# A transformer block on one core: expert multiplications, DMA issues and value products are put in another order within a step

## The chip, the core and the metric

The kernel runs on one core of one Trainium2 chip. The metric is the time of one execution on the device, in microseconds (us). TensorE (PE in the profile) multiplies matrices and loads its weights (PEld), VectorE (DVE), ScalarE (ACT) and GpSimd (POOL) work on tiles, and SyncE (SP) issues nearly all DMA transfers from one queue, in program order.

## The reference

The input x is 2 x 128 x 256 x 256 in fp32 (images, channels, rows, columns). Cut to what matters:

```python
x = x + conv(_ln_c(x))          # attention between windows
t = _to_tokens(x)               # one token for each pixel, 128 channels
t = t + ffn(_ln_t(t))           # mixture of experts

# conv: q, k, v = 1x1 convolutions (128 channels, 4 heads of 32); each 8x8 window of queries
# looks at the 12x12 window of keys around it; a mask of -inf leaves only the keys whose row
# and column offsets are of one parity; relative position logits are added
attn = softmax(q*SCALE @ k.T + rel_pos_emb(q*SCALE) + FIXED_MASK)
out  = W_out @ (attn @ v)

# ffn
router_probs = softmax(x @ router_w + router_b)      # 8 experts
top_p, top_i = top_k(router_probs, 2);  top_p /= sum(top_p)
expert_out   = einsum('bnd,edc->bnec', x, expert_w) + expert_b
out          = sum over the two chosen experts of top_p * expert_out
```

## The kernel before, in words

**Tiles.** The two images are cut into 64 strips of 8 rows. Because of the mask, queries of one parity of row and column meet only keys of that parity, so each strip splits into four planes (row parity, column parity). One step n of the main loop (line 654) handles one plane: `i, pl = divmod(n, 4)`. There are 256 steps with attention, and seven more in which the last expert work runs out.

**What a step does.** A step weaves together work of several planes and rows through generators, each `next` issuing one piece:
- `scores(n)`: position logits (L371), then scores for half of the windows (L388), then the other half, then the exponentials on ScalarE (L396). These are 32 and twice 64 short matmuls of 32 rows by 64 columns.
- `attend(n)`: the sums of the exponentials by ones (L409, 16 matmuls), the value products (L417, 128 short matmuls), then on VectorE the chain that divides by the sums: a transpose `sT` (L427), reciprocals `rc` (L429), a second transpose `rT` (L432), and the product `o` (L437).
- `out_project(n)`: `po` (L445) on TensorE, then its addition to x on VectorE (L450), the other operand being in PSUM.
- `project(n + 1)`: two copies of windows on POOL (`xcol`, L290), q (`pq`, L296), position terms (`pu`, L306, with transposes on VectorE), keys (`pk`, L325), and the values in two groups of four windows (`pvv`, L342).
- `norms` and `route` for one pair of rows (512 tokens) whose attention is finished, and `norms` for the first layer norm of a later row: transposes (`px_f`, `px_c`, L214), router logits (`plt`, L469), statistics and a chain of small VectorE operations up to the gates `g` (L535).
- `spread`: the gates are transposed (`pg`, L542), copied by ScalarE (`gT`), stored to DRAM (`gd`, L546), and read back from there as broadcasts to all 128 partitions: `rb` (L550) for the layer norm, which POOL applies in the next step (`ln1`, L264), and one `gb` of 256 KB for each expert.
- `Experts`: for each of the 8 experts, `times(e)` multiplies the rows by the broadcast gate (`xe`, L580; experts 3 and 7 on POOL, the others on VectorE) and `product(e)` adds the expert's product to the accumulator (`acc`, L585, two matmuls of 128 x 512). `end` adds the expert biases (L591) and adds the sum to x (L592); the fourth row pair of a strip also stores the strip (L612, 1 MB). Every fourth step loads a strip (L104, 1 MB).

**What sets the order.** The five engines' orders are written out by hand (`tc.manual_schedule`): what is issued first in the program comes first on its engine. The module function `times(ex, nxt, e)` issues expert e's multiplication for the rows `ex` and, behind it, the fetch of the broadcast of the same expert for the following rows `nxt`:

```python
    def times(ex, nxt, e):
        ex.times(e, pool if e % 4 == 3 else dve)
        nxt.fetch(e)
```

The fetch goes into the one buffer that the multiplication frees (`gb`, 8 buffers for 8 experts), so SP waits for the multiplication before it issues the fetch, and everything behind it in SP's queue waits too. `xe` has 6 buffers, so a multiplication waits for the product that read its buffer six multiplications earlier. In the step before the change SP's order is: the strip's load (every fourth step), `gb2`, `gb4`, `gb7`, `gb5`, `gb6`, `gd`, `rb`, `gb0`, `ge`, `gb1`, `gb3`, the strip's store (every fourth step).

Of the kernel before, what the change touches and what calls it, by code (L numbers as in the profile page):

```python
# [10 lines left out]
F32 = mybir.dt.float32  # L11
# [5 lines left out]
P = 128  # L17
# [28 lines left out]
def kernel(  # L46
# [21 lines left out]
    HP = NP // 2  # L68
# [3 lines left out]
    NT = CH // P  # L72
# [5 lines left out]
    work = ctx.enter_context(tc.tile_pool(name="work", bufs=2))  # L78
# [20 lines left out]
    def load_x(i):  # L99
        if i >= len(strips):  # L100
            return
        b, s = strips[i]
        xt[i] = xpool.tile([P, R, W], F32, tag="xt", name=f"xt{i}")
        nc.sync.dma_start(xt[i], x[b, :, s * R : (s + 1) * R, :])  # L104
# [295 lines left out]
    def attend(n, state):  # L400


        att, pT, vv = state["att"], state["pT"], state["vv"]
        av = att[:, :, HQ:512]
        for half in range(2):
            rows = slice(half * SLOT, (half + 1) * SLOT)
            for h in range(HEADS):
                hp = slice(h * DH, (h + 1) * DH)
                nc.tensor.matmul(  # L409
                    av[hp, 2 + half], lhsT=ones[rows, :], rhs=pT[rows, h], start=True, stop=True  # L410
                )
        for t in range(HP):
            for half in range(2):
                rows = slice(half * SLOT, (half + 1) * SLOT)
                for h in range(HEADS):
                    hp = slice(h * DH, (h + 1) * DH)
                    nc.tensor.matmul(  # L417
                        av[hp, half, 32 * t : 32 * t + 32],
                        lhsT=vv[rows, t, hp],
                        rhs=pT[rows, h, 32 * t : 32 * t + 32],  # L420
                        start=True,
                        stop=True,
                    )


        sT = work.tile([P, 2, HQ], F32, tag="sT", name=f"sT{n}", bufs=1)
        nc.vector.transpose(sT, av[:, 2:4])  # L427
        rc = small.tile([P, NQ // 32], F32, tag="rc", name=f"rc{n}")
        nc.vector.reciprocal(rc, sT.rearrange("p f (b k) -> p (f b) k", k=32)[:, :, 0])  # L429
        yield  # L430
        rT = work.tile([P, 2, HQ], F32, tag="rT", name=f"rT{n}", bufs=1)
        nc.vector.transpose(  # L432
            rT.rearrange("p f (b k) -> p (f b) k", k=32),
            rc.unsqueeze(2).broadcast_to([P, NQ // 32, 32]),
        )
        o = work.tile([P, 2, HQ], F32, tag="o", name=f"o{n}")
        nc.vector.tensor_tensor(o, av[:, 0:2], rT, ALU.mult)  # L437
        state["o"] = o
        yield
# [117 lines left out]
    class Experts:  # L557
# [18 lines left out]
        def times(self, e, eng):  # L576

            nm = "_".join(str(v) for v in (*self.at, e))
            self.xe[e] = work.tile([P, NT * P], F32, tag="xe", name=f"xe{nm}", bufs=6)
            eng.tensor_tensor(self.xe[e], self.src, self.gb.pop(e), ALU.mult)  # L580

        def product(self, e):
# [6 lines left out]
        def end(self):  # L589

            nc.tensor.matmul(self.acc, lhsT=eb, rhs=self.ge, start=False, stop=True)  # L591
            nc.vector.tensor_add(self.src, self.acc, self.src)  # L592
            i, k = self.at
            if k == R // 2 - 1:
                store(i)

    class NoExperts:
        def fetch(self, e):
# [7 lines left out]

        def end(self):
            pass

    def store(i):  # L610
        b, s = strips[i]
        nc.sync.dma_start(out[b, :, s * R : (s + 1) * R, :], xt.pop(i))  # L612
# [38 lines left out]

    ET = mybir.EngineType
    with tc.manual_schedule(engines={ET.PE, ET.DVE, ET.Activation, ET.Pool, ET.SP}):
        for n in range(n_planes + 7):
            i, pl = divmod(n, 4)
            live = n < n_planes
            if pl == 0:
                load_x(i + 3)
            score, attn, outp, ahead, norm, rout = none, none, none, none, none, none
            if live:  # L660
                score = scores(n, states[n])
# [12 lines left out]
            ex.product(0)  # L674
            next(score, None)
            next(ahead, None)
            times(ex, nxt, 2)
            made = next(norm, None)
            next(score, None)
            if f:  # L680
# [4 lines left out]
            next(rout, None)  # L685
            next(ahead, None)
            next(ahead, None)
            times(ex, nxt, 4)
            next(rout, None)
            if pl == 3 and i + 2 < len(strips):  # L690
                halo(i + 2)
            ex.product(1)
            times(ex, nxt, 7)
            next(attn, None)
            next(attn, None)
            if row:
                ln1(*row, pool)
            ex.product(2)
            ex.product(3)
            times(ex, nxt, 5)  # L700
            next(ahead, None)
            ex.product(4)
            next(outp, None)
            times(ex, nxt, 6)
            next(outp, None)
            next(ahead, None)
            ex.product(5)
            for c1 in cs[1:]:
                ln1_now(*c1)
            row, new = None, NoExperts()  # L710
            if made:
                gd, row = spread(f, c, made[0], f"_{n}")
                row = (*c, row) if c else None
                new = Experts(*f, gd) if f else new
            ex.product(6)
            ex.product(7)
            for e in (0, 1, 3):
                times(nxt, new, e)
            ex.end()
            ex, nxt = nxt, new  # L720
# [59 lines left out]
```

## Time and profile before

| what | value |
|---|---|
| median of 3 runs | 5573.74 us (5567.08 to 5577.78) |
| the profiled execution's own time | 5572.79 us |
| its span, first to last instruction | 5571.0 us |
| mean granted TensorE clock | 0.973 |
| busy: PE, DVE, ACT, POOL | 94%, 78%, 23%, 28% |
| DMA | 763.81 MB, mean 137 GB/s; the program's queue q1 43.0% of 16 engines' time, instruction queues q8 and q14 0.9% |
| DMA issues of a step | 8 `gb` of 256 KB, `rb` of 256 KB, `gd` of 34 KB, `ge` of 16 KB; every fourth step a load and a store of 1 MB |

The profile is one execution. A line of a group reads: source line, engine, operation, output <- inputs, sizes, count | busy time, mean ns of one | idle time of the engine just before them and what ended it. "issue" means that the engine waited for nothing that the profile shows. In a timeline, a line has start, duration, engine, line, operation, and in brackets the idle time before it. A busy TensorE is not TensorE at its peak: matmuls overlap, and their ends are modelled.

### The profile page before, as it was taken

How to read it: one execution, taken by the hardware profiler on the slowest of the kernel's cores; microseconds unless marked ns; L12 is line 12 of the kernel's file. 1: busy time of each engine (PE TensorE's matmuls, PEld its weight loads, DVE VectorE, ACT ScalarE, POOL GpSimd, SP SyncE). 2: the span in 40 equal slices, each digit the busy share in tenths (PEclk: the TensorE clock that was granted, in tenths of full speed). 3: DMA queues.
4: the chain of work that ended last, by engine and by line, in shares of the span. 5: the costliest groups of instructions: out<-in, count | busy, mean ns of one | idle time of the engine just before them, and what ended most of it. 6: DMA issues, size and time to landing. Idle time of an engine off the chain costs nothing.

```text
span 5571.0 us, 211360 instructions
## 1 busy us (share of the span) xinstructions
PE 5244.7 (94%) x93746; PEld 2980.8 (54%) x93746; DVE 4332.0 (78%) x11635; ACT 1304.3 (23%) x2845; POOL 1580.9 (28%) x1355
## 2 busy tenths in 40 slices
PE   6999999999999999999999999999999999999998
PEld 4555555555555555555555555555555555555553
DVE  5877787878777777787777788877777877787876
ACT  2222222222222222222222222222222222222221
POOL 2222323222223222232222223222222232323221
PEclk8999999999999999999999999999999999999999
DMA  1444444444444444444444444444444444444444
GB/s 59 132 136 143 137 140 138 146 139 136 149 137 140 136 145 136 140 135 145 129 135 140 136 149 144 135 145 134 137 137 137 147 141 133 137 147 142 129 130 151
DMA packets 375133, 763.81 MB, mean 137 GB/s; under 512 B 42850, under 2 KB 61898, under 8 KB 357834
## 3 DMA queue, kind: packets, MB, share of 16 engines
q1 hardware_dynamic: 371712, 749.36, 43.0%
q8 instruction: 734, 12.03, 0.8%
q14 instruction: 181, 1.48, 0.1%
q10 hardware_dynamic: 2506, 0.94, 0.1%
HBM read 674.12 MB, written 76.01 MB: 135 GB/s over the span
## 4 chain that ended last, share of the span: by engine, by line
PE 93%; issue 5%; DVE 2%; DMA 0%; ACT 0%; ACTq 0%; DVEq 0%
PE acc L585 33%; PE pvv L342 8%; PE att L388 7%; PE pk L325 7%; PE att L417 6%; PE pq L296 5%; PE acc L591 5%; PE pu L306 4%; PE po L445 4%; PE att L371 3%; PE att L409 3%; PE px_f L214 3%; PE px_c L214 2%; PE plt L469 2%; PE plg L500 1%
## 5 line engine op out<-in xcount | busy, mean ns | idle before, releaser
L585 PE MATMUL acc<-xe,ew 128*128 128x512 f32 x4096 | 2074.8, 613 | 17.6 <-DVE xe L580 9.6
L580 POOL TENSOR_TENSOR xe<-xt,gb 128x512 f32<-128x512 f32 x512 | 668.0, 1305 | 3141.1 <-PE acc L585 3138.0
L580 DVE TENSOR_TENSOR xe<-xt,gb 128x512 f32<-128x512 f32 x1536 | 1273.2, 856 | 0.7 <-PE acc L585 0.7
L585 PEld LDWEIGHTS acc<-xe,ew 128*128 128x128 f32 x4096 | 687.2, 193 | 507.1 <-issue 316.4
L349 ACT COPY vv<-pvv 128x512 f32<-128x512 f32 x512 | 300.1, 586 | 1893.8 <-PE pvv L342 1893.8
L342 PEld LDWEIGHTS pvv<-wt,xcol 128*128 128x128 f32 x4096 | 546.5, 194 | 251.7 <-issue 251.2
L264 POOL TENSOR_TENSOR xn<-xt,rb 128x512 f32<-128x512 f32 x248 | 413.7, 1668 | 788.5 <-DMA rb<-gd 788.5
L388 PEld LDWEIGHTS att<-qs,kcol 32*64 32x64 f32 x32768 | 431.0, 131 | 344.6 <-issue 344.6
L388 PE MATMUL att<-qs,kcol 32*64 32x32 f32 x32768 | 467.7, 225 | 146.3 <-issue 146.3
L592 DVE TENSOR_TENSOR xt<-acc,xt 128x512 f32<-128x512 f32 x256 | 177.1, 692 | 493.8 <-issue 442.8
L342 PE MATMUL pvv<-wt,xcol 128*128 128x128 f32 x4096 | 549.5, 278 | 2.1 <-issue 2.1
L417 PE MATMUL att<-pT,vv 64*32 64x32 f32 x32768 | 366.4, 200 | 74.0 <-issue 72.6
L325 PE MATMUL pk<-xn,wt 128*128 128x390 f32 x1024 | 416.1, 531 | 15.0 <-issue 9.9
L417 PEld LDWEIGHTS att<-pT,vv 64*32 64x32 f32 x32768 | 358.5, 105 | 118.9 <-issue 82.4
L290 POOL COPY xcol<-xn 128x480 f32<-128x480 f32 x512 | 417.6, 844 | 12.5 <-PE pvv L342 12.4
L325 PEld LDWEIGHTS pk<-xn,wt 128*128 128x128 f32 x1024 | 212.7, 208 | 241.7 <-issue 173.8
L332 ACT COPY kcol<-pk 128x480 f32<-128x480 f32 x512 | 286.6, 560 | 209.2 <-PE pk L325 187.7
L396 ACT ACTIVATE pT<-att 128x1024 f32<-128x1024 f32 x256 | 261.9, 1023 | 217.9 <-PE att L388 217.9
L477 ACT COPY lT<-plt 128x128 f32<-128x128 f32 x256 | 67.8, 265 | 995.0 <-PE plt L469 995.0
L306 PE MATMUL pu<-xn,wrel 128*128 128x512 f32 x512 | 291.0, 652 | 5.0 <-issue 3.9
L296 PE MATMUL pq<-xn,wt 128*128 128x512 f32 x512 | 289.1, 646 | 0.0
L591 PE MATMUL acc<-ge,eb 8*128 8x512 f32 x512 | 287.8, 641 | 0.0
(2948 smaller groups left out, 5779.5 us busy)
## 6 DMA issues: line engine op xcount, KB each, us to landing
gb<-gd SPq DMA_DIRECT2D x2048, 256.0 KB
xt<-in_x_dram SPq DMA_DIRECT2D x64, 1024.0 KB
out_dram<-xt SPq DMA_DIRECT2D x64, 1024.0 KB
rb<-gd SPq DMA_DIRECT2D x248, 256.0 KB
gd<-gT SPq DMA_DIRECT2D x244, 34.0 KB
ge<-gd SPq DMA_DIRECT2D x256, 16.0 KB
ew<-in_L_ffn_expert_w_dram ACTq DMA_DIRECT2D x1, 512.0 KB
gd<-gT SPq DMA_DIRECT2D x12, 32.0 KB
```

The costliest lines, as they stand in the source:

```text
L264: eng.tensor_tensor(xn[i % 2][:, :, :, k, 1 : PC + 1], ln1_src(i, k).rearrange("p (y j x) -> p y x j", y=2, x=2), rb.rearrange("p (y j x) ...
L290: nc.gpsimd.tensor_copy(xl[:, :, half, 0:NK].rearrange("p t (r c) -> p t r c", c=KC), windows(xp, half * HP, HP),)
L296: nc.tensor.matmul(pq, lhsT=wq, rhs=inner, start=True, stop=True)
L306: nc.tensor.matmul(pu, lhsT=wrel, rhs=inner, start=True, stop=True)
L325: nc.tensor.matmul(pk[:, :nk], lhsT=wk, rhs=xp[:, r : r + 3, :].rearrange("p r c -> p (r c)"), start=True, stop=True,)
L342: nc.tensor.matmul(pv[:, t * P : (t + 1) * P], lhsT=xl[:, t0 + t].rearrange("p a k -> p (a k)"), rhs=wv, start=True, stop=True,)
L349: nc.scalar.copy(vv[:, t0 : t0 + 4, :].rearrange("p t c -> p (t c)"), pv)
L388: nc.tensor.matmul(sc[rows, h, 32 * t : 32 * t + 32], lhsT=kk[hp, half * HP + t, :], rhs=qs[hp, m0 : m0 + 2].rearrange("p m a s -> p (m a ...
L417: nc.tensor.matmul(av[hp, half, 32 * t : 32 * t + 32], lhsT=vv[rows, t, hp], rhs=pT[rows, h, 32 * t : 32 * t + 32], start=True, stop=True,)
L580: eng.tensor_tensor(self.xe[e], self.src, self.gb.pop(e), ALU.mult)
L585: nc.tensor.matmul(self.acc, lhsT=ew[:, e, :], rhs=self.xe.pop(e), start=(e == 0), stop=False)
L591: nc.tensor.matmul(self.acc, lhsT=eb, rhs=self.ge, start=False, stop=True)
```

## The change

Four things are changed in the order of a step, and one buffer count.
- `attend` yields between the two halves of the value products, and product 2 is issued between them.
- The multiplication for expert 2 moves from behind the statistics to the end of the step before (with 0, 1 and 3). The multiplication for expert 4 moves from ahead of the gates' last part to behind `o`, followed by both `pvv` groups, `po`, multiplication 5, the addition of L450, product 4 and multiplication 6. Each takes its broadcast's fetch with it.
- `spread` comes ahead of product 5 instead of behind it.
- The strip's store is noted in `to_store` and issued in the next step, behind `spread`; the strip's load moves from the start of the step to that place too. SP's order in a step becomes `gb7`, `gb4`, `gb5`, `gb6`, `gd`, `rb`, store, load, `gb0`, `ge`, `gb1`, `gb2`, `gb3`.
- `xe` has 8 buffers instead of 6, and the loop has one more step.

```diff
@@ attend @@
         for t in range(HP):
+            if t == HP // 2:
+                yield
             for half in range(2):
@@ Experts @@
-            self.xe[e] = work.tile([P, NT * P], F32, tag="xe", name=f"xe{nm}", bufs=6)
+            self.xe[e] = work.tile([P, NT * P], F32, tag="xe", name=f"xe{nm}", bufs=8)
...
             if k == R // 2 - 1:
-                store(i)
+                to_store.append(i)
...
+    to_store = []
@@ main loop @@
-        for n in range(n_planes + 7):
+        for n in range(n_planes + 8):
             i, pl = divmod(n, 4)
             live = n < n_planes
-            if pl == 0:
-                load_x(i + 3)
...
             ex.product(0)
             next(score, None)
             next(ahead, None)
-            times(ex, nxt, 2)
             made = next(norm, None)
             next(score, None)
...
             next(rout, None)
             next(ahead, None)
             next(ahead, None)
-            times(ex, nxt, 4)
             next(rout, None)
             if pl == 3 and i + 2 < len(strips):
                 halo(i + 2)
             ex.product(1)
             times(ex, nxt, 7)
             next(attn, None)
+            ex.product(2)
+            next(attn, None)
             next(attn, None)
             if row:
                 ln1(*row, pool)
-            ex.product(2)
             ex.product(3)
+            times(ex, nxt, 4)
+            next(ahead, None)
+            next(ahead, None)
+            next(outp, None)
             times(ex, nxt, 5)
-            next(ahead, None)
+            next(outp, None)
             ex.product(4)
-            next(outp, None)
-            times(ex, nxt, 6)
-            next(outp, None)
-            next(ahead, None)
-            ex.product(5)
             for c1 in cs[1:]:
                 ln1_now(*c1)
+            times(ex, nxt, 6)
             row, new = None, NoExperts()
             if made:
                 gd, row = spread(f, c, made[0], f"_{n}")
                 row = (*c, row) if c else None
                 new = Experts(*f, gd) if f else new
+            while to_store:
+                store(to_store.pop())
+            if pl == 0:
+                load_x(i + 3)
+            ex.product(5)
             ex.product(6)
             ex.product(7)
-            for e in (0, 1, 3):
+            for e in range(4):
                 times(nxt, new, e)
             ex.end()
             ex, nxt = nxt, new
```

## The prediction, made before the changed kernel was run

> **What bounds the kernel.** First the profile's page: busy time, queues, the chain that ended last, groups.
>
> ```profile
> PE 5244.7 (94%) x93746; PEld 2980.8 (54%) x93746; DVE 4332.0 (78%) x11635; ACT 1304.3 (23%) x2845; POOL 1580.9 (28%) x1355
> ...
> q8 instruction: 734, 12.03, 0.8%
> ...
> PE 93%; issue 5%; DVE 2%; DMA 0%; ACT 0%; ACTq 0%; DVEq 0%
> ...
> L388 PE MATMUL att<-qs,kcol 32*64 32x32 f32 x32768 | 467.7, 225 | 146.3 <-issue 146.3
> ...
> L417 PE MATMUL att<-pT,vv 64*32 64x32 f32 x32768 | 366.4, 200 | 74.0 <-issue 72.6
> ```
>
> TensorE is the chain, with 5% of pauses in which it waited for nothing shown. They lie in the short matmuls, scores (L388, 146.3 us in 62 pauses) and value products (L417). Queue q8 carried 734 packets for 187492 weight loads and matmuls, 255 to a packet; counted in the trace, 81 of TensorE's 90 pauses over 1.7 us stand a multiple of 256 instructions apart. So TensorE waits for its own instructions, which come in blocks of 256; a block's packet is asked for when the block before it is entered, and its first instruction runs 0.95 + 1.4 us after that packet starts. Next, stretches around one pause:
>
> ```profile
> 2822.00:2827.00 5.00, 0.41 (x37) 0.30 (x22) 0.40 (x3) 0.35 (x1) 0.00 (x0) 0.77 0.93 372
> 2827.00:2832.00 5.00, 4.97 (x19) 2.78 (x20) 3.03 (x11) 1.83 (x4) 0.00 (x0) 0.54 0.05 16
> ```
>
> The DMA engines are 93% busy (last columns: clock, DMA share, GB/s) while TensorE stands still, and the granted clock falls to 0.54 afterwards. A step without a pause takes 19.83 us; the mean full step 21.4. Pauses plus clock cost some 400 us. Last, a step without a pause, TensorE, DVE, POOL and SP in order of time:
>
> ```profile
> 1168.06 0.66 PE L409 MATMUL att<-pT,ones 64*32 64x256 f32 x16
> 1168.52 1.34 PE L417 MATMUL att<-pT,vv 64*32 64x32 f32 x128
> 1169.79 1.98 PE L585 MATMUL acc<-xe,ew 128*128 128x512 f32 x4
> ...
> 1173.36 1.06 PE L445 MATMUL po<-o,wt 128*128 128x512 f32 x2
> ...
> 1177.93 1.12 PE L591 MATMUL acc<-ge,eb 8*128 8x512 f32 x2
> ```
> ```profile
> 1170.71 0.70 DVE L427 STREAM_TRANSPOSE sT<-att 128x512 f32<-128x512 f32 x1
> ...
> 1173.09 2.36 DVE L580 TENSOR_TENSOR xe<-xt,gb 128x512 f32<-128x512 f32 x2
> ```
> ```profile
> 1173.61 1.29 POOL L580 TENSOR_TENSOR xe<-xt,gb 128x512 f32<-128x512 f32 x1 [10.75 <-PE acc L585]
> ```
> ```profile
> 1176.60 0.26 SPq L546 DMA_DIRECT2D gd<-gT  x1
> 1178.60 0.32 SPq L550 DMA_DIRECT2D rb<-gd  x1
> ```
>
> Two multiplications took 2.36 us where 0.68 each is usual: one that starts during POOL work ends 0.55 us after that work (567 of 1536 such).
>
> **The multiplications' new place.** Count from the first sum matmul, 0. Value products in halves: 0.46 to 1.10, product 2 to 2.05 (0.95, as product 1 takes ahead of L409), second half to 2.69, against 2.64 for the same work: +0.05. sT starts 0.16 after the next matmul does, 2.85; by the trace's starts rc is 0.74 later, rT 0.29, o 0.74 and takes 0.69, to 5.31. po starts 0.147 after o (seven waits in the trace): 5.46, where TensorE, through product 3 (0.91) and both pvv groups (0.89 each), is free at 5.38: +0.08.
>
> Now 4, 5 and 6 come behind o. DVE starts what follows 0.61 after o's start: xe4 could run from 5.23. POOL's xe3 waits for product 3's buffer (eight buffers, one for each expert), 1.11 after that product starts: 3.80 to 5.04; xcol's first copy runs to 5.63 and blocks xe4 to 6.18; the second gets its turn to 6.63 and blocks xe5 to 7.18. The trace shows such turns where xcol meets xe. The add of L450 reads PSUM, isn't blocked (0.69 in 249 meetings), and ends 7.79; xe6 (0.61 behind the add's start, 0.68 long) 8.40. TensorE: po, p4 at 6.33, pg 7.19, p5 7.33, p6 free at 8.19 but xe6 counts from 8.55: +0.36. Step: 0.05 + 0.08 + 0.36 = 0.49; 250 full steps: +122 us. Were nothing blocked, xe6 would end at 7.86 and 0.13 remain, +32; were xe5 to lose a turn more, 0.67, +168. I take 122: turns are what the trace shows. In 62 steps halo stands behind xcol and takes a turn ahead of xe6, from xe5's end to 8.13 (0.95 in such a turn of the trace); xe6 then ends 8.68, 0.28 later: +17. Costed at nothing: xe2, which leaves the start of the step, follows xe0 and xe1 behind xe6 and ends 10.2, and L592 can't start before L591 has ended, 11.5 (DVE idles 1.56 us there today; without that cover 0.61 a step). pg ahead of product 5: its gates are done by 2.4, and pvv's copies on ScalarE end before it. rb lands 3.9 us after its issue, so ln1 comes some 0.5 us later on POOL, 5.0 to 6.5 after L591, while DVE waits for plg until 7.0. The load goes out five steps ahead of its first use instead of six; the stored strip is not read again. The extra step is empty, and the tail's seven keep their order.
>
> **Value products in halves.** 67 pauses fell in blocks of 256 that will hold product 2 between the halves; each shrinks by up to the 0.75 to 0.95 us it takes: -41 to -48 us. I take -45.
>
> **The DMA queue.** SP's order becomes gb7, gb4, gb5, gb6, gd, rb, store or load, gb0, ge, gb1, gb2, gb3. gb6 waits for xe6, so goes at 8.42, gd right behind it. Today rb goes 3.1 us after gb6 (gd must land behind it): now 11.5, with L591 at 10.36. So rb leaves 1.15 us after L591 starts (0.4 to 0.7 today), and gb0 to gb3 and gb7 follow 0.4 apart, to 3.7: not in the long products, but in the transposes, product 0 and the first scores, which start 3.5 after L591. What is queued by the scores' fetch decides. Today its packet starts 2.1 us (median) after the block is entered, 3.0 and 3.7 in steps with a 1 MB load or store; with an idle queue, 1.0. A transfer issued 1.2 us or less before the fetch doesn't hold it up: where 1 MB is issued 2.5 us after L591, blocks entered by 3.7 have their packet by 6.9, those entered from 3.77 on between 7.1 and 9.2. At 3.6, then, rb, gb0 and perhaps gb1 are ahead, where rb, gb0, gb1 and gb3 are today. A broadcast alone is done 2.95 us after its issue, each behind it 0.8 later: today 5.75 (four), then 4.9 (two) to 5.7 (three). I take 0.7 us less, near the two, in 33 pauses in and behind the scores: -23. With 1 MB, which is now issued ahead of the broadcasts and not behind them, 0.2 less in 35: -7. Sum -30; with all six ahead +60, with one broadcast fewer -80. The blocks entered from the scores' end on (31 us of pauses today) stand behind the longer queue: +10 (0 to +30).
>
> The Trainium skill ("DMA: Bandwidth & Descriptors", Queues, rings and completion order) lets a DMA engine alternate between rings by packet, so a fetch would pass the backlog. The medians of 2.1 to 3.7 us contradict it; by it the -30 and +10 would be 0.
>
> **Clock.** It was halved for 297 us in all, a loss of 149. Of pauses of 1.8 to 2.2 us 13 of 28 had it fall, over 3 us all 14. With pauses some 0.7 shorter a few fewer: -15 (-50 to +30).
>
> The skill's "Runtime: NRT & Kernel Launch" (Instruction fetch mechanics) holds fetches to be hidden by the issue rate. L388's 146.3 us deny that here; by it only the waits, +139, would be left.
>
> **Sum.** 122 + 17 - 45 - 30 - 15 + 10 = +59 us on the profiled execution's 5572.8 (span 5571.0; median of the runs 5573.7, the same within 0.02%): 5632 us.
>
> **Rivals.** *Multiplications not blocked* (faster). If POOL's xcol runs ahead of xe4 or yields, 0.13 a step: 32 - 45 - 30 - 15 + 10 = -48: 5525. For it: DVE sometimes won its turn against POOL's xe3; against: 567 blocked ones. It decides once the wait ahead of p6 is under 0.1 us. 0.15.
>
> *The scores' fetch finds an empty queue* (faster). If gd lands so late that rb leaves 2.5 us or more after L591, the fetch of 3.6 is alone: 62 pauses of 2.36 become about 0.8 (2.6 us for the block against 1.0 + 0.95 + 1.4 us of fetch), -97, the clock gives back 80: 139 - 45 - 97 - 80 + 10 = -73: 5500; with the first rival too, 5400. For it: gd stands closer behind gb6 than before. Against: 1.15 by the rows. 0.12.
>
> *The burst is all in front of the fetch* (slower). If rb leaves by 0.6, gb0 to gb3 and gb7, two more than today, are ahead: +60, clock +30, later blocks +30: 139 - 45 + 120 = +214: 5787. For it: six broadcasts now go in one run. 0.23. The change's claim, issue beside long products, would then hold for the issue alone and not for the data.
>
> **Numbers.** The forecast has 0.50, with its own range 5575 to 5690 by the bounds of its terms; of it 0.05 lies within 0.2% (11 us, what a measurement can tell from no change), the rest slower. Faster 0.15 + 0.12 = 0.27; slower 0.45 + 0.23 = 0.68; same 0.05. Range 5480 to 5760: it leaves out about half of the second and third rival.
>
> **What would show it.** Right: waits of product 6 for xe on DVE of 0.2 us or more a step; L417's pauses under 45 us in all; rb issued about 1.2 us after L591; L388's pauses 90 to 150 us; a step without a pause at 20.2 to 20.5 us. Wrong: that step at 19.9 (no blocking), or L388's pauses under 60 us (the queue was empty), or over 190.

## The result, and the profile after

The changed kernel takes 5923.74 us (median of 4 runs, 5913.18 to 5932.58), the kernel before 5575.76 on the same chip (5567.08 to 5592.32): a ratio of 1.062, 95% interval 1.0589 to 1.065. The forecast was slower, 5632 us, with a range to 5760; the loss is 348 us, six times the 59 that the sum gave. The profiled execution took 5920.86 us, its span is 5919.1 us. In the new file the scores are still L388; the other lines shown of before move by two: L417 is L419, L580 is L582, L585 is L587, L591 is L593, L546 is L548; the store's L612 is L616.

The page's lines that answer to those of before, with the products' group:

```profile
PE 5423.2 (92%) x93746; PEld 2963.7 (50%) x93746; DVE 4454.0 (75%) x11635; ACT 1306.1 (22%) x2845; POOL 1542.3 (26%) x1355
...
q8 instruction: 735, 12.04, 0.8%
...
PE 68%; DVE 27%; issue 5%; ACT 0%; DMA 0%; POOL 0%; ACTq 0%; DVEq 0%
...
L587 PE MATMUL acc<-xe,ew 128*128 128x512 f32 x4096 | 2175.9, 628 | 214.6 <-DVE xe L582 208.8
...
L388 PE MATMUL att<-qs,kcol 32*64 32x32 f32 x32768 | 467.1, 225 | 141.0 <-issue 141.0
...
L419 PE MATMUL att<-pT,vv 64*32 64x32 f32 x32768 | 419.7, 199 | 49.9 <-issue 48.9
```

The chain has changed hands: DVE, 2% of it before, has 27%, and the 5% of "issue" are still there. The products, which waited 9.6 us for multiplications on DVE before, wait 208.8. Their line on the page of before:

```profile
L585 PE MATMUL acc<-xe,ew 128*128 128x512 f32 x4096 | 2074.8, 613 | 17.6 <-DVE xe L580 9.6
```

The scores' pauses are nearly what they were (146.3 before), the value products' are down from 72.6 to 48.9. The view of stretches shows a pause as before: full DMA engines while TensorE stands still, and a lower clock behind it (the last three columns are clock, DMA share and GB/s).

```profile
3002.00:3007.00 5.00, 2.67 (x138) 1.76 (x122) 2.04 (x5) 1.00 (x3) 1.50 (x1) 1.00 1.00 328
3007.00:3012.00 5.00, 3.78 (x15) 2.04 (x16) 2.58 (x9) 1.81 (x3) 0.00 (x0) 0.71 0.33 120
```

So the time isn't in the pauses. A step without a pause takes 21.48 us where it took 19.83. Here is one in order of time, first TensorE from the first half of the value products on, then DVE and POOL around product 6, then SP's start of the step:

```profile
3103.14 0.80 PE L419 MATMUL att<-pT,vv 64*32 64x32 f32 x64
3103.87 1.12 PE L587 MATMUL acc<-xe,ew 128*128 128x512 f32 x2
3104.93 0.76 PE L419 MATMUL att<-pT,vv 64*32 64x32 f32 x64
3105.61 1.12 PE L587 MATMUL acc<-xe,ew 128*128 128x512 f32 x2
3106.57 1.95 PE L342 MATMUL pvv<-wt,xcol 128*128 128x128 f32 x16
...
3109.28 1.07 PE L587 MATMUL acc<-xe,ew 128*128 128x512 f32 x2
...
3110.30 1.05 PE L587 MATMUL acc<-xe,ew 128*128 128x512 f32 x2
3112.31 1.98 PE L587 MATMUL acc<-xe,ew 128*128 128x512 f32 x4 [0.96 <-DVE xe L582]
```
```profile
3110.09 0.68 DVE L452 TENSOR_TENSOR xt<-po,xt 128x512 f32<-128x512 f32 x1
...
3110.44 1.27 POOL L582 TENSOR_TENSOR xe<-xt,gb 128x512 f32<-128x512 f32 x1 [0.81 <-PE acc L587]
...
3110.70 1.56 DVE L582 TENSOR_TENSOR xe<-xt,gb 128x512 f32<-128x512 f32 x1
```
```profile
3093.99 0.32 SPq L552 DMA_DIRECT2D rb<-gd  x1
3094.36 0.42 SPq L616 DMA_DIRECT2D out_dram<-xt  x1
3094.88 0.38 SPq L571 DMA_DIRECT2D gb<-gd  x1
```

Products 4 (3109.28), 5 (3110.30) and 6 (3112.31) stand behind each other, and product 6 waits 0.96 us for multiplication 6. That one took 1.56 us instead of 0.68: POOL had begun multiplication 7 at 3110.44, 0.26 us before it, and it ended 0.55 us after POOL did. POOL's line says why it ran there: it had waited for a product, and went on 1.16 us after product 4 had begun. A second loss is in the first five lines: from the first value product to the matmul behind product 3 (pvv, 3106.57) it is now 3.43 us where it was 3.09 (10.40 to 13.49 us after L591 in a step without a pause of before). SP's lines show rb leaving 1.25 us after L593, which began at 3092.74, with the store and gb0 behind it.

**Where the 348 us are.** For the steps 8 to 244 of each kernel the mean step is cut into pauses in the attention's matmuls, time lost to the lower clock, and the rest, which holds all waits for another engine:

| kernel | mean step | pauses | clock | rest |
|---|---|---|---|---|
| before | 21.42 | 0.88 | 0.49 | 20.05 |
| after | 22.84 | 0.76 | 0.47 | 21.61 |
| difference, times 250 steps | +355 | -30 | -5 | +390 |

### The profile page after: what moved, and what is told of

Read it like the earlier page. It is cut to its first block, busy times and chain, and to the rows that moved or that the text cites. A ratio compares the mean times of both kernels' runs of the same rounds, so it can differ in the third digit from the quotient of the medians.

```text
span 5919.1 us, 211097 instructions
## 1 busy us (share of the span) xinstructions
PE 5423.2 (92%) x93746; PEld 2963.7 (50%) x93746; DVE 4454.0 (75%) x11635; ACT 1306.1 (22%) x2845; POOL 1542.3 (26%) x1355
## 4 chain that ended last, share of the span: by engine, by line
PE 68%; DVE 27%; issue 5%; ACT 0%; DMA 0%; POOL 0%; ACTq 0%; DVEq 0%
PE acc L587 22%; DVE xe L582 14%; PE att L388 7%; PE pk L325 6%; PE att L419 6%; PE pq L296 5%; PE acc L593 4%; PE pu L306 4%; DVE sT L429 3%; DVE rT L434 3%; DVE o L439 3%; PE att L371 3%; PE att L409 3%; PE px_f L214 3%; DVE xt L452 2%
## 5 line engine op out<-in xcount | busy, mean ns | idle before, releaser
L587 PE MATMUL acc<-xe,ew 128*128 128x512 f32 x4096 | 2175.9, 628 | 214.6 <-DVE xe L582 208.8
L582 DVE TENSOR_TENSOR xe<-xt,gb 128x512 f32<-128x512 f32 x1536 | 1405.4, 966 | 0.5 <-PE acc L587 0.5
L582 POOL TENSOR_TENSOR xe<-xt,gb 128x512 f32<-128x512 f32 x512 | 679.8, 1328 | 2481.0 <-PE acc L587 2430.4
L587 PEld LDWEIGHTS acc<-xe,ew 128*128 128x128 f32 x4096 | 664.7, 191 | 958.4 <-DVE xe L582 656.1
L264 POOL TENSOR_TENSOR xn<-xt,rb 128x512 f32<-128x512 f32 x248 | 372.7, 1503 | 1835.1 <-DMA rb<-gd 1823.8
L388 PEld LDWEIGHTS att<-qs,kcol 32*64 32x64 f32 x32768 | 430.9, 131 | 340.8 <-issue 340.8
L388 PE MATMUL att<-qs,kcol 32*64 32x32 f32 x32768 | 467.1, 225 | 141.0 <-issue 141.0
L342 PEld LDWEIGHTS pvv<-wt,xcol 128*128 128x128 f32 x4096 | 497.1, 192 | 122.4 <-issue 122.0
L419 PEld LDWEIGHTS att<-pT,vv 64*32 64x32 f32 x32768 | 383.7, 106 | 282.0 <-issue 246.3
L342 PE MATMUL pvv<-wt,xcol 128*128 128x128 f32 x4096 | 499.9, 275 | 1.7 <-DVE rc L431 0.9
L419 PE MATMUL att<-pT,vv 64*32 64x32 f32 x32768 | 419.7, 199 | 49.9 <-issue 48.9
L429 DVE STREAM_TRANSPOSE sT<-att 128x512 f32<-128x512 f32 x256 | 183.5, 717 | 369.2 <-PE att L419 369.2
L325 PE MATMUL pk<-xn,wt 128*128 128x390 f32 x1024 | 429.2, 544 | 14.4 <-issue 11.0
L506 DVE TENSOR_TENSOR lg<-plg,rs 128x32 f32<-128x32 f32 x256 | 49.0, 192 | 414.5 <-PE plg L502 414.1
```

Of the source, the lines that this page charges most:

```text
L264: eng.tensor_tensor(xn[i % 2][:, :, :, k, 1 : PC + 1], ln1_src(i, k).rearrange("p (y j x) -> p y x j", y=2, x=2), rb.rearrange("p (y j x) ...
L325: nc.tensor.matmul(pk[:, :nk], lhsT=wk, rhs=xp[:, r : r + 3, :].rearrange("p r c -> p (r c)"), start=True, stop=True,)
L342: nc.tensor.matmul(pv[:, t * P : (t + 1) * P], lhsT=xl[:, t0 + t].rearrange("p a k -> p (a k)"), rhs=wv, start=True, stop=True,)
L388: nc.tensor.matmul(sc[rows, h, 32 * t : 32 * t + 32], lhsT=kk[hp, half * HP + t, :], rhs=qs[hp, m0 : m0 + 2].rearrange("p m a s -> p (m a ...
L419: nc.tensor.matmul(av[hp, half, 32 * t : 32 * t + 32], lhsT=vv[rows, t, hp], rhs=pT[rows, h, 32 * t : 32 * t + 32], start=True, stop=True,)
L587: nc.tensor.matmul(self.acc, lhsT=ew[:, e, :], rhs=self.xe.pop(e), start=(e == 0), stop=False)
```

## The experiments

All ratios are to the kernel before on the same chip, whose medians there were 5609.6 (first four runs), 5614.5 (next four), 5618.5 and 5609.6 us. The summary comes first; "clean" is the commonest step without a pause, the pauses are those of the page's groups, the clock is the mean granted one. The pauses and the clock of before are from the first chip; on the others it took 34 to 43 us longer, with a mean clock of 0.966 to 0.974 in its runs, so small differences of these columns from that row say nothing.

| kernel | us | ratio (95%) | clean step | scores' pauses | value products' pauses | clock |
|---|---|---|---|---|---|---|
| before | 5575.76 | 1 | 19.83 | 146.3 | 72.6 | 0.973 |
| after | 5923.74 | 1.062 (1.0589 to 1.065) | 21.48 | 141.0 | 48.9 | 0.976 |
| xe7 with its own buffer | 5783.60 | 1.0309 (1.0288 to 1.033) | 20.60 | 147.5 | 65.5 | 0.976 |
| halves alone | 5669.51 | 1.011 (1.0077 to 1.0142) | 20.22 | 154.0 | 55.9 | 0.969 |
| DMA places alone | 5514.05 | 0.9822 (0.9798 to 0.9847) | 19.82 | 123.0 | 68.0 | 0.976 |
| multiplications alone | 5775.11 | 1.0292 (1.0264 to 1.0321) | 19.8 to 20.0 | 159.4 | 131.9 | 0.961 |
| after, without halves | 5722.50 | 1.0195 (1.0165 to 1.0226) | 19.8 to 20.5 | 152.9 | 103.0 | 0.964 |
| two products between | 5908.03 | 1.0527 (1.0498 to 1.0556) | 21.29 | 151.5 | 37.7 | 0.977 |
| late broadcasts | 5471.59 | 0.9746 (0.9716 to 0.9776) | 19.82 | 111.6 | 55.3 | 0.978 |
| late store and load too | 5339.64 | 0.9519 (0.9495 to 0.9542) | 19.82 | 78.9 | 22.9 | 0.988 |
| two groups of buffers | 5296.71 | 0.9428 (0.9409 to 0.9447) | 19.8 to 20.9 | 18.0 | 15.4 | 0.996 |
| the same, issued early | 5526.46 | 0.9828 (0.9798 to 0.9858) | 19.82 | 11.9 | 187.7 | 0.976 |
| store and load in pieces | 5230.56 | 0.9318 (0.9293 to 0.9342) | 19.82 | 17.9 | 6.8 | 0.993 |

### Multiplication 7 with a buffer of its own

The changed kernel, with the multiplications' eight buffers in two groups. It then waits for its own product of the step before, 7, as the prediction had assumed.

```diff
-            self.xe[e] = work.tile([P, NT * P], F32, tag="xe", name=f"xe{nm}", bufs=8)
+            own = e == 7
+            self.xe[e] = work.tile(
+                [P, NT * P], F32, tag="xe7" if own else "xe", name=f"xe{nm}", bufs=1 if own else 7
+            )
```

> The changed kernel, with one buffer for xe7 alone and seven for the other multiplications, so that POOL's xe7 waits for product 7 again, as the prediction had assumed. Theory (the buffer that xe7 gets is the one product 4 frees, so xe7 runs on POOL in the middle of VectorE's multiplications 5 and 6 and blocks xe6 by about 1.05 us a step): the step without a pause falls from 21.48 to 20.3 to 20.6 us and the time to 5630 to 5690 us; L587's pauses on xe fall from 209 us to under 110. Rival (VectorE's own order, behind o and the addition of L452, makes the waits, whatever POOL does): 5870 to 5930 us, pauses on xe as before.

The waits of this kernel, where the changed one had 208.8 us in 245 waits, and in one step the multiplication 6 right behind the addition, in order of time:

```profile
PE acc L590 <- DVE xe L585: 33.5, 64, 3.7
```
```profile
3397.34 0.68 DVE L585 TENSOR_TENSOR xe<-xt,gb 128x512 f32<-128x512 f32 x1
```

Multiplication 6 takes 0.68 us again, the clean step falls by 0.88 us, and the rest of the mean step by 0.63 (21.61 to 20.98), or 158 us in 250 steps. So the collision is shown, and which buffer brought it: with eight buffers of one group a multiplication gets the one that was left earliest, and for 7, on POOL, that is product 4's. The clean step and the waits came out as the theory had them, the time did not: 5783.6 us is 94 above its range, and 174 us of loss remain, so there is more. (33.5 us is only the matmul's own wait; its weights' load waits too. In a clean step products 5 to 7 still take 3.05 us, where they take 2.67 with nothing in the way: 0.38.)

### One part alone: halves, DMA places, multiplications

Three kernels, each the one before with one part of the change. The halves:

```diff
         for t in range(HP):
+            if t == HP // 2:
+                yield
...
             next(attn, None)
+            ex.product(2)
+            next(attn, None)
             next(attn, None)
             if row:
                 ln1(*row, pool)
-            ex.product(2)
```

> The kernel before with the value products in two halves and product 2 between them, nothing else. Theory (the changed trace shows 9.94 to 12.87 for sums, value products and product 2 where the kernel before takes 9.94 to 12.58, so the split costs 0.29 us a step, 72 us in all, and gives back about 45 us of fetch pauses and some clock): 5575 to 5605 us, step without a pause 20.1 us, L417's pauses 72 us down to 30 or less. Rival (the split costs 0.05 us a step as predicted): 5520 to 5550 us, step 19.9 us.

Slower by 1.1%, above both ranges: the split costs more than either theory gave it, and the value products' pauses do not fall to 30. The clean step grows by 0.39 us, the rest of the mean step by 0.38. In the trace from the first sum matmul to the first pvv it is 3.89 us and was 3.55, and everything behind, po at 15.61 for 15.24, is later by as much. The value products' pauses shrink from 72.6 to 55.9 us. The clock, 0.969 to 0.974 in the four runs, is no different from that of before on this chip, 0.967 to 0.973.

The places of the DMA issues (`store` and `load_x` as in the change):

```diff
-            if pl == 0:
-                load_x(i + 3)
...
-            ex.product(5)
             for c1 in cs[1:]:
                 ln1_now(*c1)
             row, new = None, NoExperts()
             if made:
                 gd, row = spread(f, c, made[0], f"_{n}")
...
+            while to_store:
+                store(to_store.pop())
+            if pl == 0:
+                load_x(i + 3)
+            ex.product(5)
```

> The kernel before with spread ahead of product 5 and the strip's store and load behind it, so that both go out ahead of gb0, gb1 and gb3; multiplications and value products as before. Theory (the same bytes leave at nearly the same time, rb 0.4 to 0.7 us after L591, and the scores' fetch meets the same queue): 5555 to 5595 us, L388's pauses 125 to 160 us. Rival (1 MB ahead of the broadcasts holds every later fetch up): 5620 us or more, L388's pauses over 190 us.

Faster by 1.8%: this part of the change is a gain, which neither the theory nor the rival had. The clean step stays, the scores' pauses fall by 23 us, the pauses behind blocks entered in the course of the scores from 49 to 24, and the clock is 0.976 to 0.979 in its runs, where before has 0.967 to 0.973 on this chip.

The multiplications' places, with eight buffers:

```diff
-            times(ex, nxt, 2)
...
-            times(ex, nxt, 4)
...
             ex.product(3)
+            times(ex, nxt, 4)
+            next(ahead, None)
+            next(ahead, None)
+            next(outp, None)
             times(ex, nxt, 5)
-            next(ahead, None)
+            next(outp, None)
             ex.product(4)
-            next(outp, None)
             times(ex, nxt, 6)
-            next(outp, None)
-            next(ahead, None)
             ex.product(5)
...
-            for e in (0, 1, 3):
+            for e in range(4):
```

> The kernel before with the multiplications alone moved as in the change (2 at the end of the step, 4 to 6 behind o, both pvv groups and po with them, eight buffers). Theory (this part alone carries the loss, through xe7 on POOL and the chain from sT to xe6): 5830 to 5900 us, step without a pause 21.1 to 21.3 us, the change's less the split. Rival (the halves or the DMA order are needed for the loss): under 5750 us.

Slower by 2.9%, but the theory that this part alone carries the loss fell: the clean step is 19.8 to 20.0 us, not 21.1 to 21.3, and the rest of the mean step is 20.28 for 20.05. Most of the loss is in pauses and clock. Each multiplication takes its fetch with it, so gb0 to gb3 and gb7 now go out in one run, and the load with them. When a block is entered in the first half of the scores, the next one's packet now starts 4.0 to 4.7 us later in every plane; before, it did so after 1.8 to 2.0 us in two of the four planes. That block is just in time, but the one behind it is then late too: its packet starts 1.1 us after the entry in every plane, for 0.4 to 0.6 in those two, and the value products pay, 131.9 us of pauses for 72.6.

The three parts alone add up to 60 - 96 + 165 = about 130 us; together they lose 348 on the first chip. The parts work on each other.

### The change without the halves

The changed kernel with the value products in one piece, products 2 and 3 behind them (the reverse of the halves' diff).

> The changed kernel with the value products in one piece again, everything else as changed. Theory (interaction): without the split, sT comes 0.4 us earlier, multiplication 6 starts before the POOL multiplication 7 does (as it does with the multiplications alone: 17.5 against 17.8 us into the step) and isn't blocked by it. A step without a pause: 19.8 to 20.1 us; waits of product 6 under 50 us in all; time 5650 to 5760. Rival (the collision belongs to the multiplications' places and the eight buffers alone, the split has no part in it): a step without a pause at 20.9 to 21.1 us, waits of product 6 near 200 us, time 5800 to 5860.

As the first theory had it: 5722.5 us, waits of product 6 for DVE of 41.3 us. In a step of its trace, multiplication 6 on DVE (the first of two in its line, 0.68 us) and POOL's multiplication 7:

```profile
3824.65 2.35 DVE L580 TENSOR_TENSOR xe<-xt,gb 128x512 f32<-128x512 f32 x2
3824.82 1.63 POOL L580 TENSOR_TENSOR xe<-xt,gb 128x512 f32<-128x512 f32 x1 [0.24 <-PE acc L585]
```

DVE is first by 0.17 us and isn't held up; in the changed kernel it was second by 0.26. The halves turn that order round: with product 2 ahead of the second half, `sT` starts 0.97 us later than without (3.05 against 2.08 us after the first sum matmul, medians of all steps) and multiplication 6 starts 0.81 later, but POOL's 7 only 0.28. So the collision needs all three: the buffer of product 4, the multiplications behind `o`, and the halves. The clean step is less even than expected, 19.8 to 20.5.

The run also shows what the halves bring within the change. Without them, 89 us of pauses lay behind blocks entered between the scores and the value products, with them 35: -54, more than the 45 forecast. They cost 1.33 us a step in the rest, 20.28 to 21.61.

### Two products between the value products

The kernel before, with the value products cut at a half and at three quarters, product 2 in the first gap and product 3 in the second.

```diff
+            if t in (HP // 2, 3 * HP // 4):
+                yield
...
             next(attn, None)
+            ex.product(2)
+            next(attn, None)
+            ex.product(3)
+            next(attn, None)
             next(attn, None)
             if row:
                 ln1(*row, pool)
-            ex.product(2)
-            ex.product(3)
```

> The kernel before, with the value products in three parts (a half and two quarters), product 2 after the first and product 3 after the second. Theory (each product put between short matmuls costs time of TensorE, some 0.3 to 0.4 us, as the halves alone showed): a step without a pause at 20.5 to 20.6 us, 0.3 to 0.4 over the 20.22 with one split, and the time, with somewhat shorter pauses, 5710 to 5790. Rival (the 0.39 us of one split came only from the later start of the chain of the sums, which po waits for, and a second split costs as little as I forecast, 0.05): a step at 21.1 us, because product 3's 0.9 us then stands ahead of the chain as well, with TensorE waiting for o; the gap ahead of po tells the two apart: none by the theory (TensorE is busy to po), 0.5 us or more by the rival.

The rival was right on the main point: a gap ahead of `po`, and a step of 21.29 us where it said 21.1. The time, 5908.0 us, is above the theory's range. In order of time, both splits and `po` of a clean step:

```profile
3201.36 1.12 PE L587 MATMUL acc<-xe,ew 128*128 128x512 f32 x2
3202.41 0.36 PE L419 MATMUL att<-pT,vv 64*32 64x32 f32 x32
3202.70 1.13 PE L587 MATMUL acc<-xe,ew 128*128 128x512 f32 x2
3203.75 0.36 PE L419 MATMUL att<-pT,vv 64*32 64x32 f32 x32
...
3206.91 1.10 PE L447 MATMUL po<-o,wt 128*128 128x512 f32 x2 [0.85 <-DVE o L439]
```

TensorE waits for `o` here, 223 us in all. From the first sum matmul to the first pvv it takes 3.87 us, against 3.89 with one split: in sum the second split costs TensorE nothing, the first 0.34, and my theory of a step of 20.5 to 20.6 us fell. Yet by the starts there is a price for each: a product between value products takes 1.05 us, twice here, where products 2 and 3 behind each other took 1.82 together in the step of before. What hides the second one is that the 32 value products behind each product take 0.29 us, while the 64 behind the one split take 0.68 (2995.55 to 2996.23 in the halves' trace). Why the 32 go faster isn't settled. What is shown is that with one split the whole step behind it is later by 0.38.

### The broadcasts later

The DMA places again (that run was the gain), and more of the queue moved away from the scores. First the broadcasts of experts 0, 1 and 3, then the store and the load too:

```diff
             times(ex, nxt, 7)
+            for e in (0, 1, 3):
+                nxt.fetch(e)
...
             for e in (0, 1, 3):
-                times(nxt, new, e)
+                nxt.times(e, pool if e % 4 == 3 else dve)
```

> The kernel before with spread ahead of product 5 and the strip's store and load behind it (as in the run with the DMA places alone), and the broadcasts of experts 0, 1 and 3 not behind their multiplications but behind gb7 of the next step, 11.7 us into it. Theory (what is queued ahead of the scores' fetch sets its pause): in steps without a store or load only rb is ahead, and the pauses of the scores fall from about 1.5 to 0.8 us each there; L388's pauses 60 to 100 us (123 with the DMA places alone), with a higher granted clock; time 5380 to 5480. Rival (the broadcasts at 11.7 us meet the fetch that the value products need, and give back what the scores gain): value products' pauses 100 us or more, time 5490 to 5560.

> As the run before it in this list, and the strip's store and load behind the three late broadcasts too, so that rb alone is ahead of the scores' fetch in all steps. Theory: L388's pauses 40 to 70 us, clock lost under 90 us, time 5300 to 5420. Rival (the 1 MB transfers, 4 us each, then hold up gd and rb, which move into the scores' window, or meet the fetch for the value products): L388's pauses over 80 us or value products' over 90, and time no better than with the late broadcasts alone.

Both times came out as the theory had them, 5471.6 and 5339.6 us, but not its picture of the queue. The scores' pauses, 111.6 and 78.9 us, are above what it gave, and SP's order of time in the second kernel shows why:

```profile
2895.71 0.32 SPq L550 DMA_DIRECT2D rb<-gd  x1
2896.12 5.93 SPq L569 DMA_DIRECT2D gb<-gd  x4
```

A step begins at 2895.7 here, and three of these four broadcasts go out by 2897.1: they are 2, 4 and 7, which took the buffers that 0, 1 and 3 had left, and had nothing to wait for. So four broadcasts, rb and these three, were still ahead of the scores' fetch. Its packet started 5.4 us after L591 (median). The trace's DMA packets show what it waited for: when it starts, 3.97 broadcasts' worth of data (256 KB each) has been moved of the 4 issued ahead of the block's entry (median). My rule (a broadcast done 2.95 us after its issue, each one behind it 0.8 later) gives 6.0 with rb issued at 0.65, its median: too late by 0.6.

That led to the next two: the broadcasts' buffers in two groups, so that 2, 4 and 7 must wait for their own multiplications, and the same with 0, 1 and 3 issued behind gb4 instead of gb7.

```diff
-            self.gb[e] = gates.tile([P, NT * P], F32, tag="gb", name=f"gb{nm}", bufs=8)
+            own = e in (0, 1, 3)
+            self.gb[e] = gates.tile(
+                [P, NT * P],
+                F32,
+                tag="gbs" if own else "gb",
+                name=f"gb{nm}",
+                bufs=3 if own else 5,
+            )
```

> As the run with the late broadcasts and the late store and load, with the broadcasts' eight buffers in two groups: three for experts 0, 1 and 3, five for 2, 4, 5, 6 and 7. In that run three broadcasts (2, 4 and 7) took the buffers that 0, 1 and 3 had just left and went out 0.4 to 1.3 us after L591, ahead of the scores' fetch, whose packet started at 5.4; now 2 and 4 must wait for their multiplications (6 and 6.7 us) and 7 for its own (11.7), so that rb alone is ahead. Theory (each broadcast ahead of the fetch holds it up by some 0.8 us, and an empty queue leaves 1.0 + 0.95 + 1.4 us of fetch against 2.65 us of block): the packet of the scores' fetch starts 4.6 to 5.0 us after L591, L388's pauses 45 to 65 us (78 there), time 5270 to 5330. Rival (what is left of the scores' pauses is the fetch's own latency, and six broadcasts from 6 to 12 us hold up the value products' fetch): L388's pauses over 70 us or value products' over 60 (20 there), time 5340 to 5420.

> As the run before it in this list, with the broadcasts of experts 0, 1 and 3 behind gb4 (6.7 us after L591) instead of behind gb7 (11.7). Theory (a fetch entered at 4.5 to 6 us has 5 to 6 us of block to hide in, the one entered at 10 to 11 us only 2.6 to 3.1): five broadcasts between 6 and 11 us cost the first nothing and leave the second's queue as it is; L417's pauses 15 to 40 us, time within 0.4% of the run before it. Rival (the fetch entered at 5 to 6 us starts up to 3 us later, and with it the next one, which the value products need): value products' pauses 60 us or more and a time 0.5 to 1.5% longer than the run before it.

The pages' lines of the scores in the first and of the value products in the second:

```profile
L388 PE MATMUL att<-qs,kcol 32*64 32x32 f32 x32768 | 457.3, 224 | 18.0 <-issue 18.0
```
```profile
L417 PE MATMUL att<-pT,vv 64*32 64x32 f32 x32768 | 362.2, 200 | 187.7 <-issue 187.7
```

With rb alone ahead (in the two planes behind 1 MB, rb itself leaves only 2.9 to 3.5 us after L591), the scores' pauses are 18.0 us where 146.3 were, well under the theory's 45 to 65, the fetch's packet starts 3.3 to 4.2 us after L591, earlier than its 4.6 to 5.0, and the kernel is 5.7% faster than before. Issued five microseconds earlier, three of the same transfers take 4.0 of these 5.7 points back. The rival had the mechanism right, 11.9 us of pauses in the scores and 187.7 in the value products, but the loss against the run before is 4.3%, not its 0.5 to 1.5. When a block is entered between the scores and the value products, the next one's packet now starts 2.0 to 2.3 us later, against -0.5 to 0.5 in the run before, and the block lasts only 2.6 to 3.3 us. The packet's place, 11.9 to 12.4 us after L591, is near where the last of five broadcasts from 6.1 on is done by the same rule, an estimate: 6.1 + 2.95 + 4 x 0.8 = 12.25. By the DMA packets, 4.4 to 4.7 of the five have been moved when it starts (medians of the planes).

What remained in the better of the two were the planes with 1 MB: `po` waited 54.8 us for `o`. The last kernel cuts the load and the store into a row pair for each step:

```diff
+        for k in range(R // 2) if part is None else [part]:
...
+            y = s * R + 2 * k
+            nc.sync.dma_start(xt[i][:, 2 * k : 2 * k + 2, :], x[b, :, y : y + 2, :])
...
-            if k == R // 2 - 1:
-                to_store.append(i)
+            to_store.append((i, k))
...
-            if pl == 0:
-                load_x(i + 3)
+            load_x(i + 3, pl)
```

> As the run with the buffers in two groups, with the strip's load and store cut into four pieces of 256 KB, one row pair each, so that each step moves one piece of either kind instead of 1 MB in two steps of four. Theory (in the steps with 1 MB the transfer, 4 us, holds up gb5 and gb6 and through them o's followers and po, whose gap before it was 43 us in all, and the fetch of the scores): a step without a pause at 19.8 us in all four planes (20.3 and 20.8 there in the planes with 1 MB), the gap ahead of po under 15 us, time 5230 to 5265. Rival (eight transfers of 256 KB from 11.7 us on last to the end of every step, so that gd and rb are late in all of them instead of in half): scores' pauses over 40 us (18 there), time 5300 to 5360.

It is the fastest, 5230.56 us, 6.8% below the kernel before (0.9293 to 0.9342), and its theory held: the clean step is 19.82 us in all four planes, and `po` waits 14.4 us for `o`. From its page:

```profile
PE 5126.0 (98%) x93746; PEld 2938.4 (56%) x93746; DVE 4038.9 (77%) x11635; ACT 1278.9 (24%) x2845; POOL 1371.3 (26%) x1355
...
PE 97%; DVE 2%; issue 1%; DMA 0%; ACT 0%; ACTq 0%; DVEq 0%; SPq 0%
...
L391 PE MATMUL att<-qs,kcol 32*64 32x32 f32 x32768 | 459.7, 224 | 18.1 <-issue 17.9
...
L420 PE MATMUL att<-pT,vv 64*32 64x32 f32 x32768 | 348.1, 200 | 7.6 <-issue 6.8
```

"issue" is 1% of the chain where it was 5%, and the mean step 19.99 us, 0.17 above the clean one. None of the change's moves of multiplications or value products is in this kernel; it holds the orders of before on TensorE, DVE and POOL, but for product 5, which now stands behind `pg`. Otherwise only the transfers' places and sizes and the broadcasts' buffers differ.

## Why the prediction was right or wrong, by its steps

**The sign was right, the size was not.** The sum was +59; the loss was 348. By terms, with the mean steps above (the forecast of the rest, 122 + 17 us, is 0.56 a step):

| term | forecast, us | measured, us | from |
|---|---|---|---|
| split of the value products | 0.05 x 250 = +13 | 0.38 x 250 = +95 | halves alone |
| waits for xe4 to xe6, po, halo | (0.44 x 250) + 17 = +127 | 0.55 x 250 = +138 | own buffer less halves alone, rest 20.98 - 20.43 |
| collision with multiplication 7 | none | 0.63 x 250 = +158 | after less own buffer |
| all pauses | -45 - 30 + 10 = -65 | -30 | mean steps |
| clock | -15 | -5 | mean steps |

The measured column adds up to 356 us, against 355 between the mean steps, because it must: its rows are differences along one row of kernels, from before over the halves and the own buffer to the change. Along another the shares differ: taken out of the whole change, the halves cost 1.33 us a step, not 0.38, since the collision goes with them. The second row is what is left between two kernels, not a run of its own.

**The step that failed most** is the sentence "eight buffers, one for each expert". It was read from a count, not from the order in which buffers come free. A buffer goes to the next multiplication that asks, so with the new order 7 got product 4's, ran on POOL 1.16 us after that product's start, and held up 6. The sum had nothing for this; it took 0.63 us a step. The trace of before could have warned that buffers don't go round by count. With six buffers, "six multiplications earlier" would have let 7 start behind product 6; in the step shown it started behind product 7 (products 6 and 7 are the first line's four matmuls):

```profile
1176.12 1.88 PE L585 MATMUL acc<-xe,ew 128*128 128x512 f32 x4
```
```profile
1178.08 1.27 POOL L580 TENSOR_TENSOR xe<-xt,gb 128x512 f32<-128x512 f32 x1 [1.65 <-PE acc L585]
```

Taken in the order in which they were left, the six buffers give 7 product 7's there, and the eight give it product 4's. My rule of blocked multiplications priced the rest correctly. The ends forecast for 4, 5 and the addition, 6.18, 7.18 and 7.79 us after the first sum matmul, came out as 6.50, 7.50 and 8.10 in the changed kernel (medians), all late by the same 0.3; and 6 ended 0.55 us behind POOL's 7.

The Trainium skill ("SBUF — State Buffer", SBUF: two separate sides) calls the port pair that VectorE and GpSimd share an exclusive lock, held by whichever instruction starts first, for its whole length. The traces agree: 1.56 us for multiplication 6 behind a POOL start 0.26 earlier, 0.68 where DVE starts alone or first. Behind the rule stands a lesson that the prediction missed: a shift of 0.8 us of multiplication 6 decided who was first.

**The split** was mis-sized, +0.05 for 0.38. I took the spans of neighbouring groups from a run without a split and added one switch. The skill's "TensorEngine Tiling (Array Packing)", Tiling Modes, says that changing the tiling mode drains TensorE, and gives no price. The rows fit in so far as each product between 64-row matmuls takes 1.05 us, but that a drain is the cause isn't shown, and the sum of the second split (-0.02 us after 0.34 for the first) doesn't show a price for each.

**Product 6's wait** was right: 0.36 was forecast, and 0.38 is there once multiplication 7 is out of the way. The clean step was to be 20.2 to 20.5 us; with the own buffer it is 20.60, over it by less than the split's unforeseen 0.33.

**The halves' gain of 45** was right as a mechanism (-54 with and without the halves, the rest as changed), but the longer burst gave much of it back. The term for later blocks was +10, with 30 as its end; the change without halves shows +42 (blocks entered in the course of the scores: 49 to 61; behind them: 59 to 89).

**The scores' gain of 30 wasn't there.** The pauses behind blocks entered up to the start of the scores went from 155.6 to 160.7 us. rb's issue came as forecast, 1.25 us after L593 (3093.99 against 3092.74) for 1.15. What failed is the count of what is ahead of the fetch: "rb, gb0 and perhaps gb1". Its packet started at 6.3 to 6.7 us (medians of the planes, blocks entered 3 to 4 us after L593). In the planes without 1 MB, four broadcasts, rb to gb2, had been issued by 2.75 us, rb at 1.06; by my rule they are done at 1.06 + 2.95 + 3 x 0.8 = 6.41, two of them at 4.8. So a broadcast issued 0.9 us before the fetch is still ahead of it.

**The signs.** Three of the five signs of being right came, product 6's wait, rb's issue and L388's 141 us; L388's would have come with nothing gained there too. L417's pauses (48.9 for under 45) and the clean step didn't.

**Rivals.** *Multiplications not blocked* would have been nearly right on product 6's wait without the halves (41.3 us in all), though 4 and 5 were blocked there too, and wrong on the time, since pauses grew. *The scores' fetch finds an empty queue* didn't happen in this change, but its mechanism is shown by the two groups of buffers: forecast 5500, or 5400 with no multiplication blocked, and 5297 measured where only rb was ahead and the multiplications stayed. *The burst in front of the fetch* had the size nearest to the result, 5787, by the wrong cause.

## What to carry to other kernels

Before a multiplication is moved, follow which buffer it will get and whose reader it will then wait for; a pool of as many buffers as users doesn't give each user its own. Where an engine pauses for nothing that the profile shows, look at its instruction queue's packets: here they stood behind data transfers, and what matters is how many transfers have been issued by the time a block is entered, against how long that block lasts. A transfer needs a wait to stay late: when the broadcasts of 0, 1 and 3 were taken out of the early queue, those of 2, 4 and 7 found free buffers and went out in their place.

## What the runs showed that I had not expected

- With only rb ahead, or an older transfer done, the fetch's packet starts from 0.4 us before to 0.5 us after its block's entry (medians of the planes in the two kernels with the buffers in two groups, for blocks entered 3 to 4 us after L591), not the 1.0 that I had taken for an idle queue; so with an empty queue the pauses nearly vanish, where I had reckoned 0.8 us each.
- A late fetch makes the next one late. In the kernel before, the packet asked for between the scores and the value products starts 0.4 to 0.6 us after the block's entry in the planes without 1 MB ahead of the scores, and 1.1 in the two with it; the pauses behind these blocks are 14 us in the former and 45 in the latter, though the 1 MB is done by then.
- The clock gives back more than half as much as the pauses do: from the kernel before to the last one the attention's pauses fell from 219 to 25 us, and the time lost to a lower clock (one less the granted clock, summed over the span) from 148 to 34.
